# Two graph layers on one core: where the seven block products of a pair of row tiles stand among the adjacency matmuls of layer 0

## The chip, the core and the metric

The kernel runs on one core of a Trainium2 chip. The metric is the device time of one execution in microseconds (us). One more execution was taken by the hardware profiler; all rows quoted below are of that one. The engines are TensorE (PE; its weight loads are shown as PEld), VectorE (DVE), ScalarE (ACT), GpSimd (POOL) and SyncE (SP, which here only issues DMAs). PSUM is the accumulator memory that TensorE writes and ACT and DVE read.

## The reference

N = 3327 nodes, 1024 features. Two layers, each with a layer norm and a relu ahead of it and a residual sum behind it. Cut to what matters here:

```python
# layer 0
h = jnp.maximum(_layernorm(x), 0.0)
support   = relu(matmul(quant(h), quant(weight)) * scales)        # N x 1024
support_q = quant(support)
x = x + matmul(adj / asf, support_q / delta) * asf * delta        # (N x N) @ (N x 1024)
# layer 1: eight attention heads of 64 features, then four dense layers
h  = jnp.maximum(_layernorm(x), 0.0)
Wh = jnp.einsum('nf,hfd->hnd', h, W)                              # N x 512 over all heads
e  = leaky_relu(e_src[:, :, None] + e_dst[:, None, :])            # e_src = Wh . a1, e_dst = Wh . a2
att = softmax(where(adj > 0, e, -9e15))
enc = concat_heads(elu(att @ Wh))
x = x + dense4(enc)
```

The change lies in the product Wh = h W of layer 1, which the kernel computes during the adjacency product of layer 0.

## The kernel before

**Stages.** The rows are padded to 26 tiles of 128. First the support of layer 0 is made (to about 125 us). Then comes the adjacency stage (125.6 to 887.8 us), which is where the change is. Then attention over 8 heads and 4 groups of tiles, and at the end the dense layers.

**The adjacency stage** is a loop over the 26 row tiles t (line 820). For each, an accumulator `mm` of 128 x 1024 (two PSUM banks, two buffers) sums over the 26 column tiles j. Each adjacency block is split into a high part (`hi`, a cast by ACT, line 192) and a rest (`lo`, a subtraction by DVE, line 196), and each part is multiplied with both 512-column halves of `s_int[j]`: four matmuls for a j, 104 for a tile (line 849). The column tiles come in seven parts, `PARTS`: 0-3, 4-7, 8-11, 12-15, 16-19, 20-22, 23-25. A part is loaded by one DMA on SP's queue (line 188) into `at`; `at`, `hi` and `lo` have three buffers each, so the cast of a part waits until TensorE is done with the part three before it. DVE also makes the mask bytes `mk` from each part (line 197).

When a tile's sum is complete, ACT empties it (line 870), DVE scales it, adds it to x, measures it and normalises it (lines 871, 872, 148 to 153), ACT splits the row into two planes (line 626), two transposing DMAs on SP's queue turn it (line 628), and ACT joins the planes to `ht` (line 636). The next load of x and of adjacency parts stand behind those transposes in SP's queue.

**The pair of heads.** Wh for two neighbouring row tiles is computed in one 2 x 2 block product of Strassen's kind: seven block products in place of eight. `combined` (line 673) makes the sums of the stationary blocks on DVE, and `pair_of_heads` (line 693) is a generator that issues the seven products, the sums over them, and `closing_of_heads`. This happens in each even tile t from 2 to 24 (`paired`), for the tiles t-2 and t-1: 12 pairs.

A block product (`product`, line 704) is 4 float32 matmuls of 128 x 256, which the trace shows as 8 passes on TensorE. The results go to tiles `products` of one PSUM bank each (2 x 256 floats), two buffers. Product 1 opens a tile and product 2 takes its second half; 6 opens the second tile and 3 takes its second half; 7 opens one again (the first buffer) with 5 in its second half; 4 opens the second buffer again. Their readers:

- ACT copies product 1 to `p1` (line 718).
- DVE (line 716 is the helper `plus`) makes the first half of `wht` from p1 and product 2, then `u2` from p1 and product 6, then the second half of `wht` from u2 and product 3, then p1 anew from u2 and product 7, then adds product 5 to the second half.
- Then the tile t-2's rows are scaled and closed (line 730, `closing_of_heads` at line 790, with the scores, the exponentials on ACT, and the features `fw`, written by POOL's queue at line 813); the tile t-1's follow in the next tile.

**The order.** The instructions of an engine run in program order, and a scheduler sets that order from dependences and its own costs; `tc.keep_in_program_order` pins an instruction against its neighbours, and `queue_behind(ins, other)` (line 156) says that `ins` stands behind `other` in the engine's queue, with no semaphore.

In the loop over the parts n and their column tiles q, the generator is advanced (`next(steps)`) at (n, q) = (5, 1), (5, 2), (6, 0) and (6, 1). In the order that is built, product 1 stands behind the first column tile of part 5, and between the products stand adjacency matmuls, three and one in turn:

`1, three, 2, one, 6, three, 3, one, 7, three, 5, one, 4`

Of the kernel before, what the change touches and what calls it, by code (L numbers as in the profile page):

```python
# [28 lines left out]
KF = F // P  # L29
# [39 lines left out]
def two_layer_kernel(  # L69
# [23 lines left out]
    nc = tc.nc  # L93
# [34 lines left out]
    def load_rows(dst, ap, t):  # L128

        if rows_of(t) < P:  # L130
            nc.gpsimd.memset(dst, 0.0)
        for r in row_pieces(t):
            nc.sync.dma_start(dst[r], ap[t * P + r.start : t * P + r.stop, :])
# [22 lines left out]
    def queue_behind(ins, other):  # L156

        tc.add_manual_dep(
            ins.ins,
            other.ins.name,  # L160
            mybir.DependencyInfo(mybir.DependencyClass.NoSync, mybir.DependencyReason.DATA),
            reason="queue_behind",
        )
# [11 lines left out]
    with tc.tile_pool(name="at", bufs=2, reuse_waits="tile") as atp:  # L175
# [47 lines left out]
        with tc.tile_pool(name="s1", bufs=2, reuse_waits="tile") as s1, tc.tile_pool(  # L223
# [9 lines left out]
            def pin(ins):  # L233
                tc.keep_in_program_order(ins)

            def small_ps(name):
                return mm_ps.tile([P, F], F32, tag="mm", name=name)
# [106 lines left out]
            def product(t, c, k):  # L344
                if c == 0 and k == 0:
                    mms[t] = mm_ps.tile([P, F], F32, tag="mm", name="mm")
                r = slice(c * 512, (c + 1) * 512)
                pin(
                    nc.tensor.matmul(  # L349
                        mms[t][:, r], xqts[t][:, k, :], w_int[:, k, r], start=(k == 0), stop=(k == KF - 1)  # L350
                    )
                )
                if c == FC - 1 and k == KF - 1:
                    del xqts[t]
# [84 lines left out]
            ps = small_ps("w_meanp")  # L439
# [160 lines left out]
        with tc.tile_pool(name="differences", bufs=1, reuse_waits="tile") as dp, tc.tile_pool(  # L600
# [68 lines left out]
            def weight_differences():  # L669
                for d, one, other in ((t3, b22, b12), (b12, b12, b11), (t2, b22, b12), (t4, b21, t2)):  # L670
                    nc.vector.tensor_tensor(d, one, other, ALU.subtract)
# [21 lines left out]
            def pair_of_heads(t, of):  # L693

                r0, r1 = scales.pop(t), scales.pop(t + 1)
                wht = s2.tile([P, EMB], F32, name="wht", bufs=1)
                p1 = s2.tile([P, EMB // 2], F32, name="p1", bufs=1)
                u2 = s2.tile([P, NH, 2, HC], F32, tag="ft", name="u2", bufs=1)
                u2 = u2.rearrange("p h q c -> p (h q c)")[:, : EMB // 2]
                order = tc.keep_in_program_order  # L700
                half = slice(0, EMB // 2), slice(EMB // 2, EMB)
                banks = []

                def product(b):
                    st, mv = of[b]
                    if b in "1674":
                        banks.append(wh_ps.tile([P, 2, EMB // 2], F32, name="products"))
                    ps = banks[-1][:, int(b in "235")]
                    for k in range(KF // 2):
                        order(  # L710
                            nc.tensor.matmul(ps, st[:, k], mv[:, k], start=(k == 0), stop=(k == KF // 2 - 1))
                        )
                    return ps

                def plus(out, one, other):
                    nc.vector.tensor_tensor(out, one, other, ALU.add)

                order(nc.scalar.copy(p1, product("1")))
                plus(wht[:, half[0]], p1, product("2"))
                yield  # L720
                plus(u2, p1, product("6"))
                plus(wht[:, half[1]], u2, product("3"))
                yield
                plus(p1, u2, product("7"))
                of_5 = product("5")
                plus(wht[:, half[1]], wht[:, half[1]], of_5)
                yield
                of_4 = product("4")
                yield
                nc.vector.tensor_scalar(wht, wht, r0, None, ALU.mult)  # L730
                closing_of_heads(t, wht)
                yield
                wht = s2.tile([P, EMB], F32, name="wht", bufs=1)
                plus(wht[:, half[1]], p1, of_5)
                plus(wht[:, half[0]], p1, of_4)
                nc.vector.tensor_scalar(wht, wht, r1, None, ALU.mult)
                closing_of_heads(t + 1, wht)
                yield
# [77 lines left out]
                return products, powers  # L816

            hts, scales = {}, {}
            steps = iter(())
            for t in range(T):  # L820
                xt = s2.tile([P, F], F32, name="xt2", bufs=1)

                with tc.issue_after(turned.ins) if turned is not None else nullcontext():
                    load_rows(xt, x, t)
                mm = mm_ps.tile([P, F], F32, tag="mm", name="mm2")
                paired = t >= 2 and t % 2 == 0
                for n, js in enumerate(PARTS):
                    hi, lo = parts.pop(0)
                    parts.append(next(columns, None))
                    if n == 3:  # L830
                        for _ in steps:
                            pass
                    if js is PARTS[-1] and t - 2 in BATCHES:
                        rows_of_scores(t - 2)
                    if t == 1 and n == 0:
                        weight_differences()
                    if t > 0 and n == (3 if paired else 5):
                        join_planes(ht, parts_of_ht)
                        queue_behind(joins[0], highs[-1])
                    if paired and n == 3:  # L840
                        of = combined(t - 2)
                    for q, j in enumerate(js):
                        if paired and (n, q) == (5, 1):
                            steps = pair_of_heads(t - 2, of)
                        if paired and (5, 1) <= (n, q) <= (6, 1):
                            next(steps)
                        for which in (hi, lo):
                            for c in range(FC):
                                nc.tensor.matmul(  # L849
                                    mm[:, c * 512 : (c + 1) * 512],  # L850
                                    which[:, q, :],
                                    s_int[j][:, c * 512 : (c + 1) * 512],
                                    start=(j == 0 and which is hi),
                                    stop=(j == T - 1 and which is lo),
                                )
                if paired:
                    next(steps)
                if t == T - 2:
                    nc.gpsimd.dma_start(
                        b12, w_heads[: F // 2, EMB // 2 :].rearrange("(k p) e -> p k e", p=P)  # L860
                    )
                if t == 0:
                    for dst, ap in (
                        (whead, w_heads.rearrange("(k p) e -> p k e", p=P)),
                        (a1_t, a1.partition_broadcast(P)),
                        (a2_t, a2.partition_broadcast(P)),
                    ):
                        tc.keep_in_program_order(nc.sync.dma_start(dst, ap))
                y = s2.tile([P, F], F32, name="y", bufs=1)
                emptied = nc.scalar.activation(y, mm, AF.Copy, scale=r_asf)  # L870
                resumed = nc.vector.tensor_scalar(y, y, asf_t, sup_delta, ALU.mult, ALU.mult)
                nc.vector.tensor_tensor(xt, xt, y, ALU.add)
                nc.gpsimd.dma_start(x1_d[t * P : (t + 1) * P, :], xt)
                _, v = normalised(y, xt)
                r = half_inverse(v, "ln")
                lacking = nc.vector.tensor_scalar(r, r, 2.0, None, ALU.mult)
                if t == T - 1:
                    break
                ht, turned, parts_of_ht = transposed_by_dma(y, t)
                hts[t], scales[t] = ht, r  # L880
# [25 lines left out]
    with tc.tile_pool(name="over", bufs=2, reuse_waits="tile") as overp, tc.tile_pool(  # L906
# [18 lines left out]
        def load_features(h, js):  # L925
            r = slice(js[0], js[-1] + 1)
            return nc.sync.dma_start(
                (f_odd if h % 2 else f_even)[:, r], feat_d[r, h].rearrange("t p c -> p t c")
            )
# [148 lines left out]
        ins = load_features(0, range(8))  # L1078
        queue_behind(ins, scores)
        with tc.issue_after(ins.ins):  # L1080
            ins = load_mask(0, slice(TH, T))
        with tc.issue_after(ins.ins):
# [5 lines left out]
            ins = load_mask(3)  # L1088
# [404 lines left out]
```

## Time and profile before

| what | value |
|---|---|
| median of 3 runs | 2084.92 us (2084.8 to 2086.4) |
| the profiled execution's own time | 2085.89 us |
| its span, first to last instruction | 2084.1 us |
| adjacency matmuls, line 849 | 125.6 to 887.8 us |
| one adjacency matmul, median start to start | 0.227 us |
| block products, line 711 | 672 passes, 191.96 to 862 us |
| a tile without a pair / with a pair | 23.58 / 35.95 us |
| granted TensorE clock | 1.00 |

A row of the timeline gives the start in us from the span's start, how long the merged instructions ran, the engine, line and operation, what it writes and reads (`out<-in`), the shape, the count, and in brackets the idle time of the engine before it and what ended that. `PE` and `PEld` are the same engine; a weight load can run while a matmul streams. A row of the windows gives the window, its length, the busy time and count of PE, PEld, DVE, ACT and POOL in it, the granted clock, the DMA engines' busy share and GB/s.

Of the page's costliest groups, the two of the adjacency stage and the matmuls of the heads' pair stand like this (line, engine, operation, operands, count, busy us, mean ns, idle before):

```profile
L849 PE MATMUL mm<-s_int,lo 128*128 128x512 f32 x1352 | 429.5, 395 | 0.0
L849 PE MATMUL mm<-s_int,hi 128*128 128x512 f32 x1352 | 426.1, 396 | 0.0
```

A mean of 395 ns against a spacing of 227 shows that matmuls overlap: what counts is the spacing.

### The profile page before, as it was taken

What the parts mean: (1) busy time and instruction counts of PE and PEld (TensorE: products, weight loads), DVE (VectorE), ACT (ScalarE), POOL (GpSimd) and SP (SyncE); (2) the same over time, 40 slices, a digit from 0 to 9 for tenths busy, and PEclk for the clock granted to TensorE, in tenths of its full rate; (3) what the DMA queues carried; (4) which work ended last, traced back from release to release, by engine and by line L of the source; (5) the groups of instructions that cost most, each with busy time, mean ns of one, the idle gap of its engine ahead of it and who ended that gap; (6) DMA issues with size and microseconds to landing.
All of it is one profiled execution on the core that took longest, in us unless ns stands there. A gap on an engine that the chain in (4) does not pass through costs nothing.

```text
span 2084.1 us, 38595 instructions
## 1 busy us (share of the span) xinstructions
PE 2049.6 (98%) x15531; PEld 1742.2 (84%) x15541; DVE 1533.4 (74%) x3032; ACT 1337.0 (64%) x1828; POOL 183.1 (9%) x279
## 2 busy tenths in 40 slices
PE   5999999999999999999999999999999999999998
PEld 2468888888888888879999999999999999855554
DVE  8845676767666777687878777878778877757666
ACT  6733555444445554498888898888898888752321
POOL 2200000000020000111000000000000000000000
PEclk9999999999999999999999999999999999999999
DMA  6744554554455554592323224132324114544322
GB/s 222 177 146 139 169 161 147 147 144 140 149 166 169 161 151 147 148 374 88 97 59 114 67 66 118 42 112 64 118 66 117 41 43 123 115 110 132 116 86 76
DMA packets 202931, 261.98 MB, mean 126 GB/s; under 512 B 106020, under 2 KB 140948, under 8 KB 202752
## 3 DMA queue, kind: packets, MB, share of 16 engines
q1 hardware_dynamic: 183660, 191.08, 32.5%
q0 software_dynamic: 19024, 68.38, 10.4%
q8 instruction: 121, 1.98, 0.4%
q14 instruction: 58, 0.48, 0.1%
q10 hardware_dynamic: 68, 0.06, 0.0%
HBM read 155.90 MB, written 79.98 MB: 113 GB/s over the span
## 4 chain that ended last, share of the span: by engine, by line
PE 54%; ACT 1%; DVE 1%; issue 0%; DVEq 0%; ACTq 0%
PE acc L1019 41%; PE o L1402 7%; PE h_ps L1321 3%; PE h_ps L1290 1%; ACT over L990 1%; PE h_ps L1188 1%; PE whm L747 0%; DVE sel L999 0%; DVE sel L1000 0%; DVE su L1038 0%; DVE su L1043 0%; DVE prod L797 0%; ACT ht L1052 0%; DVE ft L779 0%; DVE stats L148 0%
## 5 line engine op out<-in xcount | busy, mean ns | idle before, releaser
L1019 PEld LDWEIGHTS <-sel 128*128 128x128 fp8e4 x10816 | 910.6, 98 | 8.4 <-issue 3.8
L990 ACT ACTIVATE over<-srow,large_dst 128x896 uint8<-128x896 f32 (+1 forms) x766 | 683.2, 974 | 12.5 <-DVE sel L999 12.4
L1019 PE MATMUL acc<-f_even,sel 128*128 128x195 bf16 x5408 | 458.6, 248 | 2.1 <-DVE sel L1000 0.9
L1019 PE MATMUL acc<-f_odd,sel 128*128 128x195 bf16 x5408 | 456.7, 248 | 0.0
L849 PE MATMUL mm<-s_int,lo 128*128 128x512 f32 x1352 | 429.5, 395 | 0.0
L849 PE MATMUL mm<-s_int,hi 128*128 128x512 f32 x1352 | 426.1, 396 | 0.0
L999 DVE TENSOR_TENSOR sel<-over,mask 128x448 uint32<-128x448 uint32 (+1 forms) x416 | 243.8, 586 | 160.3 <-ACT over L990 130.4
L849 PEld LDWEIGHTS mm<-s_int,lo 128*128 128x128 f32 x1352 | 253.8, 188 | 52.5
L849 PEld LDWEIGHTS mm<-s_int,hi 128*128 128x128 f32 x1352 | 253.8, 188 | 51.9
L1000 DVE TENSOR_TENSOR sel<-sel,mask 128x448 uint32<-128x448 uint32 (+1 forms) x416 | 245.9, 591 | 14.2
L192 ACT CAST hi<-at 128x512 fp32r<-128x512 f32 (+1 forms) x182 | 105.6, 587 | 153.2 <-PE mm L849 95.7
L196 DVE TENSOR_TENSOR lo<-at,hi 128x512 fp32r<-128x512 f32 (+1 forms) x182 | 117.7, 647 | 35.3 <-ACT hi L192 33.8
L1052 ACT ACTIVATE ht<-su,rs 128x64 f32<-128x64 f32 x208 | 53.2, 335 | 106.4 <-DVE rs L1048 106.4
L1067 POOL DMA_DIRECT2D enc_d<-eh x64 | 57.7, 906 | 717.0 <-ACT eh L1065 716.5
L1038 DVE TENSOR_REDUCE su<-acc 128x130 f32<-128x390 f32 x208 | 115.6, 556 | 4.8 <-PE acc L1019 4.8
L349 PE MATMUL mm<-w_int,xqt 128*128 128x512 bf16 x406 | 93.3, 383 | 7.1 <-DVE w_int L480 4.5
L626 ACT COPY yh<-y 128x1024 uint16<-128x1024 uint16 x50 | 51.9, 1038 | 57.0 <-DVE y L151 57.0
L349 PEld LDWEIGHTS <-xqt 128*128 128x128 bf16 x416 | 40.4, 99 | 55.3 <-issue 8.8
L636 ACT COPY ht<-yht 128x1024 uint16<-128x1024 uint16 x50 | 67.6, 1357 | 25.4 <-DMA yht<-yh 25.1
L197 DVE TENSOR_SCALAR mk<-at 128x512 uint8<-128x512 f32 (+1 forms) x182 | 72.4, 398 | 0.0
L1043 DVE SCALAR_TENSOR_TENSOR su<-su,ratio 128x65 f32<-128x65 f32 x208 | 59.7, 287 | 7.4
L803 ACT ACTIVATE ratio<-srcs 128x8 f32<-128x8 f32 x26 | 5.4, 209 | 88.2 <-DVE srcs L798 88.2
(291 smaller groups left out, 2075.3 us busy)
## 6 DMA issues: line engine op xcount, KB each, us to landing
at<-in_adj_t SPq DMA_DIRECT2D x130, 256.0 KB, 3.1
feat_d<-fw POOLq DMA_DIRECT2D x24, 800.0 KB, 6.1
x_d<-xt POOLq DMA_DIRECT2D x26, 512.0 KB, 3.5
xb<-x_d SPq DMA_DIRECT2D x26, 512.0 KB, 3.6
x_d<-xb POOLq DMA_DIRECT2D x26, 512.0 KB, 3.4
nodes<-x_d SPq DMA_DIRECT2D x26, 512.0 KB, 4.7
xt<-in_x SPq DMA_DIRECT2D x25, 512.0 KB, 4.2
out<-yo SPq DMA_DIRECT2D x50, 256.0 KB, 2.1
```

Of the source, the lines that this page charges most:

```text
L192: ins = high = nc.scalar.copy(hi, at)
L196: low = nc.vector.tensor_tensor(lo, at, hi.bitcast(F32), ALU.subtract)
L197: ins = nc.vector.tensor_scalar(mk[:, r], at, 0.0, float(EDGE), ALU.is_gt, ALU.mult)
L349: nc.tensor.matmul(mms[t][:, r], xqts[t][:, k, :], w_int[:, k, r], start=(k == 0), stop=(k == KF - 1))
L636: nc.scalar.copy(halves_of_words(ht[:, c * KF // FC : (c + 1) * KF // FC].rearrange("p k i -> p (k i)")), yht.rearrange("p (two k) i -> p ...
L849: nc.tensor.matmul(mm[:, c * 512 : (c + 1) * 512], which[:, q, :], s_int[j][:, c * 512 : (c + 1) * 512], start=(j == 0 and which is hi), s ...
L990: nc.scalar.activation(over[:, q], srows[i], AF.Relu, bias=large_dst[:, j, h : h + 1], scale=BIG)
L999: pin(nc.vector.tensor_tensor(up, over, of_pair, ALU.bitwise_and))
L1000: ends["vector"] = pin(nc.vector.tensor_tensor(dn, up, of_pair, ALU.bitwise_xor))
L1019: ins = nc.tensor.matmul(accs[i, b][:, r], chosen[i, pair][:, s, b, q], f[:, j, s * FS : s * FS + FW // 2], start=(j == 0 and s == 0), sto ...
L1038: nc.vector.tensor_reduce(su[:, b], accs.pop((i, b)).rearrange("p (q s c) -> p q c s", q=2, s=3), AX.X, ALU.add)
L1402: nc.tensor.matmul(ps, st[:, k, q // 2], mv[:, k], start=(k == 0), stop=(k == 1))
```

## The change

In `pair_of_heads` the three `yield`s between the products go, so that one advance of the generator issues all seven. That advance stands at (n, q) = (5, 2), ahead of the last column tile of part 5. The block products' matmuls are collected in a list, and the high matmuls of that column tile and of the first column tile of each later part are queued behind the last of them. The sums over the products, the closing of the two tiles and everything else are as they were.

```diff
@@ pair_of_heads
-                order = tc.keep_in_program_order
...
                     for k in range(KF // 2):
-                        order(
-                            nc.tensor.matmul(ps, st[:, k], mv[:, k], start=(k == 0), stop=(k == KF // 2 - 1))
+                        block_products.append(
+                            tc.keep_in_program_order(
+                                nc.tensor.matmul(ps, st[:, k], mv[:, k], start=(k == 0), stop=(k == KF // 2 - 1))
+                            )
                         )
...
-                order(nc.scalar.copy(p1, product("1")))
+                tc.keep_in_program_order(nc.scalar.copy(p1, product("1")))
                 plus(wht[:, half[0]], p1, product("2"))
-                yield
                 plus(u2, p1, product("6"))
                 plus(wht[:, half[1]], u2, product("3"))
-                yield
                 plus(p1, u2, product("7"))
                 of_5 = product("5")
                 plus(wht[:, half[1]], wht[:, half[1]], of_5)
-                yield
                 of_4 = product("4")
                 yield
@@ the loop over the tiles
             hts, scales = {}, {}
+            block_products = []
...
                     for q, j in enumerate(js):
-                        if paired and (n, q) == (5, 1):
+                        if paired and (n, q) == (5, 2):
                             steps = pair_of_heads(t - 2, of)
-                        if paired and (5, 1) <= (n, q) <= (6, 1):
                             next(steps)
                         for which in (hi, lo):
                             for c in range(FC):
-                                nc.tensor.matmul(
+                                ins = nc.tensor.matmul(
...
+                                if block_products and which is hi and (q == 0 or (n, q) == (5, 2)):
+                                    queue_behind(ins, block_products[-1])
```

In the order that is built, product 1 stands behind the second column tile of part 5, and the seven products follow one another with nothing between them; the last column tile of part 5 and part 6 come behind product 4. The waits written on products 2 (for ACT), 6, 3 and 5 (for DVE) are the same as before. On DVE, the low part and mask of the next tile's second part move from among the sums to behind the first three operations of the closing, and the low parts of its fourth and fifth parts move ahead of the normalisation of the row. On ACT the cast of the next tile's third part moves ahead of the emptying of the sum. On POOL's queue two of the mask loads at the end of the stage move behind the feature write of tile 22, and the feature write of tile 23 ahead of a write of scores.

## The prediction

> **What bounds the kernel now.** I read the page's busy line first, then the busy time by window for one tile with a pair in it and one without, then the timeline of that pair on all engines, then what waits for what.
>
> ```profile
> span 2084.1 us, 38595 instructions
> PE 2049.6 (98%) x15531; PEld 1742.2 (84%) x15541; DVE 1533.4 (74%) x3032; ACT 1337.0 (64%) x1828; POOL 183.1 (9%) x279
> ```
>
> ```profile
> 232.45:268.40 35.95, 35.95 (x161) 29.92 (x160) 19.45 (x41) 12.66 (x17) 2.21 (x3) 1.00 0.48 135
> 268.40:291.98 23.58, 23.58 (x105) 19.52 (x104) 21.36 (x44) 16.93 (x25) 2.34 (x3) 1.00 0.62 182
> 125.60:887.80 762.20, 762.20 (x3381) 632.45 (x3379) 512.59 (x1035) 363.73 (x509) 68.54 (x97) 1.00 0.54 154
> ```
>
> In the window rows the second figure is PE's busy time. Over the whole of layer 0's adjacency stage (125.6 to 887.8 us) TensorE has no idle time. A tile without a pair takes 23.58 us for its 104 adjacency matmuls, 0.2267 each; the tile with a pair takes 35.95, so the pair's block products cost 12.37. Whatever lengthens TensorE's stream here moves the end by as much: nothing in this stage can pay it back, as TensorE waits nowhere else in it.
>
> The timeline of that pair (products in the order 1, 2, 6, 3, 7, 5, 4):
>
> ```profile
> 251.49 1.89 PE L711 MATMUL products<-whead,ht 128*128 128x256 f32 x8
> ...
> 253.03 0.81 PE L849 MATMUL mm<-s_int,hi 128*128 128x512 f32 x2
> 253.42 0.37 ACT L718 COPY p<-products 128x256 f32<-128x256 f32 x1 [2.46 <-PE products L711]
> ...
> 253.68 0.40 PE L849 MATMUL mm<-s_int,lo 128*128 128x512 f32 x1
> 253.84 1.59 PEld L711 LDWEIGHTS products<-whead,ht 128*128 128x128 f32 x8 [0.20 <-ACT p L718]
> 253.91 1.92 PE L711 MATMUL products<-whead,ht 128*128 128x256 f32 x8
> ...
> 255.90 1.89 PE L711 MATMUL products<-differences,s 128*128 128x256 f32 x8
> ...
> 257.83 0.42 DVE L716 TENSOR_TENSOR u<-p,products 128x256 f32<-128x256 f32 x1 [1.46 <-PE products L711]
> ...
> 258.30 1.59 PEld L711 LDWEIGHTS products<-whead,s__2469 128*128 128x128 f32 x8 [0.26 <-DVE u L716]
> 258.32 1.98 PE L711 MATMUL products<-whead,s__2469 128*128 128x256 f32 x8
> ...
> 262.77 1.59 PEld L711 LDWEIGHTS products<-whead,s 128*128 128x128 f32 x8 [0.26 <-DVE p L716]
> ```
>
> The reader is to see three weight loads that stand still until ACT or DVE has read the product before: 2 waits for the copy of 1, 3 for the sum that reads 6, 5 for the sum that reads 7. Each of these shares an accumulator tile with the product it follows. Between the two stand three adjacency matmuls, 3 x 0.2267 = 0.68 us, which cover nearly all of the wait.
>
> **The change part by part.** *The three covers go.* One product is 8 passes (x8). Its 1.89 us run from the start of the first to the end of the last, and one pass alone lasts 0.379, so passes start every (1.89 - 0.379)/7 = 0.2158 us, and a product takes 1.726 of TensorE's time. Seven make 12.08 us; the 0.285 that the pair costs above that is three waits not quite covered (1.92 and 1.98 against 1.89: 0.03 + 0.09 + 0.09 = 0.21) and about 0.075 for 14 changes between the two kinds of matmul.
>
> In the changed order the seven follow one another, still with the waits at 2, 3 and 5. The full length of each wait is in the same rows. Product 1's last pass starts at 251.49 + 7 x 0.2158 = 253.00, so a next pass could start at 253.22; ACT's copy ends at 253.79, the weights load from 253.84, and the first pass effectively starts 0.03 after its record, at 253.95: 0.73 us. Product 6: last pass at 257.41, next possible 257.63, DVE's sum ends 258.25, load 258.30, effective start 258.32 + 0.09 = 258.41: 0.78. Product 7 to 5: the same, 0.78. Sum 2.29 us. The other three changeovers wait for nothing: 6 goes to a free accumulator, 7 needs the sum of 1 and 2, which ends some 3.6 us sooner, 4 needs the sum with 3, done some 3.6 us sooner.
>
> So a pair costs 12.08 + 2.29 + two changes of kind (about 0.01) = 14.38 in place of 12.37: +2.01 us. There are 12 pairs: +24.1 us.
>
> A bound for these waits from below: if the weights of the waiting product were in place already, each would be shorter by the 0.11 us between the first and the second load after the wait, 36 x 0.11 = 4.0 us in all. From above: one mask instruction of DVE (L197, 0.42 us) in front of one of the sums, 12 x 0.42 = 5.0. I take the measured waits, because the same semaphore ends them in both kernels and DVE is idle before each sum (1.46 us before the one above).
>
> The Trainium skill, "TensorE: Matmul & The Clock Gate", section "Step-by-step: what each phase is for", says that TensorE pulls weight loads ahead of running matmuls. The rows above show 0.20 and 0.26 us in which the load of the waiting product did not go ahead, so the wait holds it too; by the rule the sum would be some 4 us smaller, about 2106.
>
> *The moved instructions.* Product 1 starts two adjacency matmul pairs (0.91 us) later, so all that reads block products starts at the same place or later than before while the tile's end is 2.0 us later: the sums end 4.7 us ahead of the tile's end (3.2 before), no new cost. The adjacency matmuls behind the piece release their high and low parts later, so the casts for the next tile's second part, in ACT's and DVE's queues behind the pair's copy and sums, run at about 267.4 in place of 258.28; TensorE wants them at 274.0. In DVE's order the pair's sums go ahead of that part's low half, and two later low halves and one mask move ahead of the normalisation (L151). From the starts of the rows, L871 to L151 was 6.39 us and becomes 6.39 + 0.60 + 0.29 = 7.28, so the normalised row, its two transposes and, behind them in SP's queue, the next xt load and adjacency loads are 0.9 to 1.0 us late relative to TensorE. The cover: the first part of tile 6 was cast by 288.58 and wanted at 291.98, 3.4 us; some 2.4 remain. In POOL's queue tile 22's feature write, which waits for DVE until 872, goes ahead of two mask loads that stood at 870 to 871: some 3 us later, first wanted by the selection at 893.30. Nothing.
>
> Only at the end of layer 0 is that cover already gone:
>
> ```profile
> 886.37 1.36 ACT L636 COPY ht<-yht 128x1024 uint16<-128x1024 uint16 x1 [3.67 <-DMA yht<-yh]
> ```
>
> The last-but-one tile's head products start at 887.78, as soon as this copy ends (887.73). A row that is 1.0 us late delays them by that, once: +1.0 us (0 to 1.6). The chain of waits goes through TensorE there, so it reaches the end.
>
> *Queueing later adjacency matmuls behind the block products* adds order, no semaphore: 0.
>
> *The clock.* New gaps of 0.73 to 0.78 us stand in TensorE's stream, three within 14 us.
>
> ```profile
> 28.30:100.00 71.70, 67.91 (x352) 31.79 (x358) 63.60 (x157) 54.21 (x61) 19.60 (x44) 1.00 0.65 170
> ```
>
> Here TensorE is idle 3.8 us out of 71.7, with one gap of 1.3 us at 68 us, and the granted clock stays at 1.00. So I take 0. The same page, section "A second HAM failure mode: psum-queue depth-cycling", tells of short idle times between groups of matmuls that make the clock fall to half; its window is 3.4 us, and by that rule an estimate is 1.7 us lost a pair, 20 us in all, about 2130.
>
> *Sum:* 24.1 + 1.0 = 25.1 us. The profiled execution has a span of 2084.1 and took 2085.89, 1.8 us around the span; the median of the runs is 2084.92. The span becomes 2109.2, the median 2110.0.
>
> **The rivals.**
> - *Not slower: the accumulators come free at once.* If the waits at 2, 3 and 5 were only the lateness of ACT and DVE behind other work, a piece would cost 12.08 + 0.01 and save 0.28 us a pair: -3.3 us, 2081.6. It decides only if the three waits together stay under 0.28 us. Against it: ACT and DVE start 0.04 us after the product's last pass ends, and the copy or sum alone takes 0.37 or 0.42. For it: only that the order of products is unchanged and was covered.
> - *The adjacency is late.* If the casts of the next tile's first part come 1 us too late (the 2.4 us cover misjudged by 3.4), TensorE waits in each pair's next tile: 12 us more, 2122. For it: ACT already waits 0.78 us for that load at 287.96. Against it: the margin.
> - *All six changeovers wait*, because each accumulator's release is told late: 3 x 0.78 more a pair, 28 us more, 2138. Against it: the sums that free them end 3.6 us sooner.
>
> **How the numbers follow.** Forecast 0.87, not slower 0.04, adjacency late 0.06, all six 0.03. Time: 2110.0. Range: down by 4.0 (weights in place) and 1.0 (no carry at the end of the layer), 2105; up by 5.0 and 0.6, 2115.5; outside it lies about 0.17. What a measurement can tell from no change is about 0.2%, 4.2 us: faster (under 2080.7) 0.01, same 0.04, slower 0.95.
>
> **What would show it.** Paired tiles of 37.96 us and odd tiles still of 23.58; PE idle before products 2, 3 and 5 of 0.7 to 0.8 us and none at 6, 7 and 4; layer 0's matmuls ending 24 us later; the granted clock at 1.00. Wrong if the piece takes under 13 us, if matmuls of L847 wait for casts, or if the loss of layer 0 doesn't arrive at the end.

## The result, and the profile after

The changed kernel takes 2110.91 us (median of 4 runs, 2108.6 to 2111.86) against 2085.55 for the kernel before beside it (4 runs, 2084.8 to 2086.4): a ratio of 1.012, with a 95% interval of 1.0102 to 1.0137. It is slower by 25.4 us; 25.1 had been forecast.

The profiled execution of after has a span of 2110.1 us. Its busy line, from the page:

```profile
span 2110.1 us, 38606 instructions
PE 2056.9 (97%) x15531; PEld 1742.9 (83%) x15541; DVE 1530.3 (73%) x3032; ACT 1336.7 (63%) x1828; POOL 179.4 (9%) x279
```

The same number of matmuls as before, 26.0 us more of span, of which the page counts 7.3 as PE busy and the rest as idle. Of the 26.0, 24.4 lie in the adjacency stage of layer 0; this profile also enters that stage 2.55 us later than the one of before, with a granted clock of 0.98 ahead of it (28.3 to 125 us; 1.00 in before), and is 1.0 us shorter behind it. The busy time by window, for the same pair's tile, the tile that follows it, and the whole adjacency stage of layer 0 (window, its length, PE busy, PEld, DVE, ACT, POOL, granted clock, DMA share, GB/s):

```profile
237.08:275.05 37.97, 36.49 (x162) 29.91 (x160) 20.37 (x45) 13.04 (x20) 2.43 (x3) 1.00 0.42 120
275.05:298.62 23.57, 23.57 (x105) 19.52 (x104) 20.86 (x41) 16.41 (x23) 2.02 (x4) 1.00 0.64 192
128.12:914.76 786.64, 768.78 (x3381) 632.61 (x3380) 510.80 (x1036) 364.90 (x510) 65.10 (x97) 1.00 0.52 149
```

The odd tile is what it was; the paired tile has gone from 35.95 to 37.97, and has idle time on PE that it did not have. All twelve paired tiles lie between 37.97 and 38.00. The stage has gone from 762.24 to 786.64 us, +24.40 by the ends of its matmuls, while PE's busy time in it has grown by 6.6: the stage lost its time in waits, of which the profile shows 17.9 us as idle and counts the rest as busy. The clock is 1.00 in each row.

Where the idle time sits is in the timeline of that pair (start, duration, engine, line, operation, and in brackets the idle time before it with its releaser):

```profile
257.02 1.89 PE L711 MATMUL products<-whead,ht 128*128 128x256 f32 x8
258.95 0.37 ACT L719 COPY p<-products 128x256 f32<-128x256 f32 x1 [3.37 <-PE products L711]
259.37 1.59 PEld L711 LDWEIGHTS products<-whead,ht 128*128 128x128 f32 x8 [0.86 <-ACT p L719]
259.37 1.99 PE L711 MATMUL products<-whead,ht 128*128 128x256 f32 x8 [0.46 <-ACT p L719]
261.20 1.89 PE L711 MATMUL products<-differences,s 128*128 128x256 f32 x8
263.13 0.42 DVE L717 TENSOR_TENSOR u<-p,products 128x256 f32<-128x256 f32 x1 [1.24 <-PE products L711]
263.61 1.99 PE L711 MATMUL products<-whead,s__2469 128*128 128x256 f32 x8 [0.51 <-DVE u L717]
265.44 1.89 PE L711 MATMUL products<-differences,ht 128*128 128x256 f32 x8
267.84 1.99 PE L711 MATMUL products<-whead,s 128*128 128x256 f32 x8 [0.51 <-DVE p L717]
269.67 1.89 PE L711 MATMUL products<-differences,ht 128*128 128x256 f32 x8
```

Seven products, in the order 1, 2, 6, 3, 7, 5, 4. Those with a bracket are 2, 3 and 5, the ones that write the other half of an accumulator that ACT or DVE is still reading. They last 1.99 instead of 1.89: with the semaphore the weight load starts at the same moment as the matmul, and its 0.10 us are part of the wait. So product 2 really starts at 259.47, 2.45 after product 1, where a product takes 1.726: a wait of 0.73. By the same reading product 3 waits 0.78 and product 5 0.77. The page's 0.46 and 0.51 are smaller because the last pass's end and the load don't count as idle.

### The profile page after: what moved, and what is told of

The parts are those of the page before. It is cut to its first block, busy times and chain, and to the rows that moved or that the text cites. A ratio compares the mean times of both kernels' runs of the same rounds, so it can differ in the third digit from the quotient of the medians.

```text
span 2110.1 us, 38606 instructions
## 1 busy us (share of the span) xinstructions
PE 2056.9 (97%) x15531; PEld 1742.9 (83%) x15541; DVE 1530.3 (73%) x3032; ACT 1336.7 (63%) x1828; POOL 179.4 (9%) x279
## 3 DMA queue, kind: packets, MB, share of 16 engines
q0 software_dynamic: 19024, 68.38, 10.2%
## 4 chain that ended last, share of the span: by engine, by line
PE 53%; ACT 2%; DVE 1%; issue 0%; DVEq 0%; ACTq 0%
PE acc L1019 40%; PE o L1402 7%; PE h_ps L1321 3%; ACT over L990 1%; PE h_ps L1290 1%; PE h_ps L1188 1%; DVE su L1038 0%; DVE sel L999 0%; DVE sel L1000 0%; DVE ft L777 0%; DVE su L1043 0%; ACT fw L785 0%; ACT ht L1052 0%; DVE prod L795 0%; DVE over L984 0%
## 5 line engine op out<-in xcount | busy, mean ns | idle before, releaser
L990 ACT ACTIVATE over<-srow,large_dst 128x896 uint8<-128x896 f32 (+1 forms) x766 | 683.1, 974 | 13.6 <-DVE sel L999 12.5
L847 PE MATMUL mm<-s_int,hi 128*128 128x512 f32 x1352 | 419.1, 391 | 0.0
L847 PE MATMUL mm<-s_int,lo 128*128 128x512 f32 x1352 | 416.5, 389 | 0.0
L847 PEld LDWEIGHTS mm<-s_int,lo 128*128 128x128 f32 x1352 | 253.8, 188 | 53.0
L847 PEld LDWEIGHTS mm<-s_int,hi 128*128 128x128 f32 x1352 | 253.7, 188 | 52.8
L626 ACT COPY yh<-y 128x1024 uint16<-128x1024 uint16 x50 | 51.9, 1038 | 61.0 <-DVE y L151 61.0
L717 DVE TENSOR_TENSOR wht<-p,products 128x256 f32<-128x256 f32 x36 | 13.9, 414 | 56.5 <-PE products L711 56.5
```

The lines of the kernel that those rows point to most:

```text
L847: ins = nc.tensor.matmul(mm[:, c * 512 : (c + 1) * 512], which[:, q, :], s_int[j][:, c * 512 : (c + 1) * 512], start=(j == 0 and which is hi),
L990: nc.scalar.activation(over[:, q], srows[i], AF.Relu, bias=large_dst[:, j, h : h + 1], scale=BIG)
```

## The experiments

In the order in which they ran; "stage" is layer 0's adjacency stage, from its first matmul to the end of its last, "behind" what follows it. Times in us; each ratio is to the kernel before, run in turn on the same chip, where its median was 2086.29 beside e1 to e4, 2086.33 beside e5 to e8 and 2086.45 beside e9.

| kernel | paired tile | stage | behind | median | ratio, 95% interval |
|---|---|---|---|---|---|
| before | 35.93 to 35.96 | 762.24 | 1196.31 | 2085.55 | |
| after | 37.97 to 38.00 | 786.64 | 1195.30 | 2110.91 | 1.012, 1.0102 to 1.0137 |
| e1, order 1 6 2 3 7 4 5 | 35.67 | 758.85 | 1198.41 | 2085.95 | 1.0, 0.9991 to 1.0009 |
| e2, order 1 6 2 3 7 5 4 | 36.45 to 36.47 | 768.28 | 1196.82 | 2093.8 (one run) | |
| e3, one sum made twice | 38.43 to 38.45 | 792.03 | 1196.08 | 2117.11 (one run) | |
| e4, nothing queued behind | 35.93 to 37.74 | 766.57 | 1194.79 | 2089.85 | 1.0017, 1.0008 to 1.0026 |
| e5, before again | 35.94 to 35.96 | 762.27 | 1195.28 | 2086.02 (one run) | |
| e6, e1 with masks moved | 35.67 | 758.83 | 1196.08 | 2084.20 | 0.9987, 0.9978 to 0.9996 |
| e7, before with masks moved | 35.95 to 35.96 | 762.26 | 1197.77 | 2088.37 | 1.0009, 1.0 to 1.0018 |
| e8, e4 at the earlier place | 35.93 to 35.95 | 761.94 | 1196.07 | 2086.56 | 0.9998, 0.9989 to 1.0007 |
| e9, e6 with features first | 35.67, one 35.85 | 759.03 | 1199.67 | 2087.82 | 1.0007, 0.9998 to 1.0016 |

The time ahead of the stage is the same program in all, and lies between 125.57 and 128.12 in these profiles. The two that enter the stage last, after and e1, have a granted clock of 0.98 ahead of it, all others 1.00. Before and before again differ by 1.1 there and by 1.0 behind the stage. Differences of that size between two profiles are therefore not explained here.

**e1: the same piece, in an order in which no product follows the one that it shares a bank with.**

```
-                banks = []
+                banks = {}
...
-                        banks.append(wh_ps.tile([P, 2, EMB // 2], F32, name="products"))
-                    ps = banks[-1][:, int(b in "235")]
+                        banks[b] = wh_ps.tile([P, 2, EMB // 2], F32, name="products")
+                    ps = banks[{"2": "1", "3": "6", "5": "7"}.get(b, b)][:, int(b in "235")]
...
-                plus(wht[:, half[0]], p1, product("2"))
                 plus(u2, p1, product("6"))
+                plus(wht[:, half[0]], p1, product("2"))
                 plus(wht[:, half[1]], u2, product("3"))
                 plus(p1, u2, product("7"))
+                of_4 = product("4")
                 of_5 = product("5")
                 plus(wht[:, half[1]], wht[:, half[1]], of_5)
-                of_4 = product("4")
```

> The changed kernel with the products in the order 1, 6, 2, 3, 7, 4, 5 (same piece, same place, same queueing; 2, 3 and 5 write the second half of the bank opened by 1, 6 and 7 as before). Now another product of 1.73 us stands between each pair that shares a bank. Theory (three waits for the reader of the first half, 0.73 + 0.78 + 0.78 us a pair): no wait is left, the paired tile takes 23.58 + 12.08 + 0.01 = 35.67 us, 2.32 less than the changed kernel's 37.99, 12 pairs 27.9 us less: about 2083, 3 us under the kernel before. Rival (the piece as such costs, by its place or by what is late behind it): it stays near 2110.

The same pair in e1, TensorE's timeline:

```profile
254.61 1.89 PE L711 MATMUL products<-whead,ht 128*128 128x256 f32 x8
256.34 1.89 PE L711 MATMUL products<-differences,s 128*128 128x256 f32 x8
258.06 1.89 PE L711 MATMUL products<-whead,ht 128*128 128x256 f32 x8
259.79 1.89 PE L711 MATMUL products<-whead,s__2469 128*128 128x256 f32 x8
261.52 3.62 PE L711 MATMUL products<-differences,ht 128*128 128x256 f32 x16
264.97 1.89 PE L711 MATMUL products<-whead,s 128*128 128x256 f32 x8
```

No bracket is left: a product every 1.72 or 1.73 us, two of them in one record of 16 passes. The stage is 27.8 us shorter than after's. So the piece costs nothing by being in one piece; the three hand-overs of a bank cost it all. The paired tile is 0.28 us below that of before, which is the 0.285 that the prediction found above pure passes in the old order. But the 3.4 us that the stage wins over before do not reach the end (ratio 1.0): behind the stage, e1 takes 2.1 us more than before, 3.1 more than before again.

**e2: the same, with 5 directly behind 7.** Against e1, `of_5` and its sum stand ahead of `of_4` again, so one wait comes back.

> As the first, but 5 directly behind 7 and 4 last: one of the three waits comes back. Theory: only product 5 waits, 0.78 us a pair, 9.4 us over the order 1, 6, 2, 3, 7, 4, 5, paired tile 36.46 us, about 2092. Rival (a wait moves to where there is most to wait for, so that one is as long as three): near 2110.

```profile
261.17 1.89 PE L711 MATMUL products<-differences,ht 128*128 128x256 f32 x8
263.57 1.99 PE L711 MATMUL products<-whead,s 128*128 128x256 f32 x8 [0.51 <-DVE p L717]
```

One bracket in the pair (TensorE's timeline of e2), 0.78 to 0.80 us a paired tile, 9.43 us over the stage; three such waits are 28.3 against the 27.8 that e1 took away. The waits add up one by one.

**e3: the sum that frees product 6's bank is made twice.**

```
-                plus(u2, p1, product("6"))
+                of_6 = product("6")
+                plus(u2, p1, of_6)
+                plus(u2, p1, of_6)
```

> The changed kernel with the sum of product 6 made twice by DVE, one behind the other, the same result. Theory: product 3's weight load waits for the last reader of product 6, so that wait grows by one sum and its hand-over, 0.42 to 0.48 us, 12 pairs: 5.0 to 5.8 us over the changed kernel, about 2116, and the waits at 2 and 5 stay. Rival (the wait is a fixed time that TensorE needs between two products of one bank): no change, about 2111.

The pair in e3, DVE and the weight load of product 3:

```profile
262.61 0.88 DVE L717 TENSOR_TENSOR u<-p,products 128x256 f32<-128x256 f32 x2 [1.24 <-PE products L711]
263.54 1.59 PEld L711 LDWEIGHTS products<-whead,s__2470 128*128 128x128 f32 x8 [1.37 <-DVE u L717]
```

DVE's 0.46 us more are TensorE's 0.46 us more: the idle time before product 3 grows from 0.91 to 1.37, the stage by 5.39 = 12 x 0.45. DVE has time enough here (1.24 us idle before it starts); what counts is how long its reading of the bank takes.

**e4: after without the queueing of later adjacency matmuls.**

```
-                                if block_products and which is hi and (q == 0 or (n, q) == (5, 2)):
-                                    queue_behind(ins, block_products[-1])
```

> The changed kernel without queueing later adjacency matmuls behind the block products; the order that is built then has three adjacency matmuls between 1 and 2, between 6 and 3 and between 7 and 5, and none elsewhere. Theory: the covers are back, each wait is down to 0.03 to 0.10 us, a paired tile takes 35.9 us and the time is that of the kernel before, 2083.5 to 2086. Rival (one advance of the generator at the later place costs by itself): near 2110, or in between.

In the order as built, three adjacency matmuls stand between 1 and 2, between 6 and 3 and between 7 and 5 again, and none elsewhere. The stage is 20.1 us shorter than after's, and eight of the paired tiles have before's 35.9. Without the two queueing lines other matmuls slip into the gaps, whatever the source says of one piece, and no product of a paired tile shows a wait any more. But the stage is still 4.3 us longer than before's, which was not expected: the kernel takes 2089.85, above the upper end of the theory. Four paired tiles take 36.47, 36.88, 37.13 and 37.74. One of them, first ACT and then TensorE in e4's timeline:

```profile
473.05 0.62 ACT L192 CAST hi<-at 128x512 fp32r<-128x512 f32 x1 [2.51 <-DMA at<-in_adj_t]
...
479.68 0.60 ACT L192 CAST hi<-at 128x512 fp32r<-128x512 f32 x1
485.71 1.05 ACT L626 COPY yh<-y 128x1024 uint16<-128x1024 uint16 x1 [5.42 <-DVE y L151]
...
489.11 1.03 ACT L192 CAST hi<-at 128x512 fp32r<-128x512 f32 x2
...
489.78 0.73 PE L847 MATMUL mm<-s_int,hi 128*128 128x512 f32 x2 [0.98 <-ACT hi L192]
```

The lateness begins at the adjacency loads: the cast of this tile's first part stands 2.51 us for its load. Behind it in ACT's order come feature casts that DVE needs, then the copy of the normalised row, for which ACT stands 5.42 us, and only then the casts that TensorE needs next. The same holds for another of the four, with the cast at 291.52:

```profile
291.52 0.62 ACT L192 CAST hi<-at 128x512 fp32r<-128x512 f32 x1 [3.39 <-DMA at<-in_adj_t]
```

In the four long tiles the first part is cast 0.22, 0.80, 1.08 and 1.49 us before TensorE wants it, in the other eight 1.99 us or more. TensorE does not wait there yet; it waits at the fifth part, whose cast stands behind the row. This is the prediction's second rival, the late adjacency, in a kernel that is not after. The later place alone does not bring it, for e1 has that place too, a pair still shorter, and no such wait (its least lead is 1.32 us); there the piece is closed. e8 below has the piece drawn apart at the old place.

**e5: before again**, for the spread between two profiles of one program.

> The kernel before once more, for a second profile of it. If the 125.6 us ahead of the adjacency stage and the 1196.3 us behind it vary by themselves, as they do between the profiles of the other kernels (126.8 to 128.1 and 1194.8 to 1198.4), this one lies inside those, and the 2.55 us by which the changed kernel's stage began later is no part of the change. If 125.6 is the kernel's own, it is 125.6 again. The stage itself: 762.2 us both ways.

The stage repeats within 0.03 us, what lies around it within 1.1.

**e8: e4 with the piece at its old place**, to tell the place from the piece: `(5, 2)` becomes `(5, 1)`.

> The changed kernel without the queueing, as in the fourth experiment, with the seven products one column tile earlier, where the kernel before has them. In the fourth experiment four of the twelve paired tiles were 0.5 to 1.8 us longer because ScalarE's casts came late. Theory (the later place takes 0.9 us of the lead that the loads behind the row's transposes have): no paired tile is longer than 36.0 us, about 2086. Rival (one advance of the generator puts DVE's order so that the row is late): the same long tiles, about 2090.

Every paired tile takes 35.93 to 35.95, TensorE waits for no cast, and the time is before's (0.9998), though the normalised row is 1.1 us later after a paired tile than in before. So the three generator stops that the change takes out are worth nothing either way. e4's 4.6 us more of stage than e8's come from the later place, and, with e1, only where the piece is also drawn apart. That this is because the piece then ends later is not shown, nor why the loads come late.

**Why e1's gain did not reach the end: e6, e7 and e9.** The first attention matmuls need a selection, and the first selection (`over`, L990 in after and e1) stands in ACT's order behind the two copies that end the last transposed rows. ACT in e1, at the end of layer 0:

```profile
885.34 1.35 ACT L636 COPY ht<-yht 128x1024 uint16<-128x1024 uint16 x1 [5.39 <-DMA yht<-yh]
...
891.63 3.84 ACT L990 ACTIVATE over<-srow,large_dst 128x896 uint8<-128x896 f32 x4
```

and in before:

```profile
891.29 3.84 ACT L990 ACTIVATE over<-srow,large_dst 128x896 uint8<-128x896 f32 x4
```

Against the end of the stage (886.88 and 887.80) the selection is later in e1: it comes 4.75 us after it, in before 3.48 and in before again 2.42. In before, after, e1, e4, e5 and e8 alike the 61st attention matmul comes 11.25 or 11.26 us after this first selection, so what moves it moves the first attention matmuls. Of the 2.1 us that e1 takes longer than before behind the stage, 1.3 are there at the selection; the other 0.8 come behind the 61st matmul and are not explained.

What makes the selection late is only in part seen. ACT stands 5.39 us for the last-but-one tile's transposes. The last of these lands 9.1 us after its issue in e1, beside seven mask loads that POOL issues, but that is no longer than in the two profiles of before (9.8 and 7.5). What is later in e1 is the row itself: its copy (L626) starts 12.78 us ahead of the stage's end, in both profiles of before 14.71 or 14.70. The same holds in the paired tiles ahead: from tile 6 to tile 22 the copy starts 10.8 us after the tile's end in e1, 9.6 in after and 8.9 in before. It is later than in before in every run with one advance of the generator (9.4 in e4, 10.0 in e8), and latest with e1's order; what puts it back on DVE was not followed up, and no run brings it forward. Instead, e6 takes e1 and moves the mask loads to SP's queue, behind the score row:

```
-        load_mask(0, slice(0, TH), nc.gpsimd)
...
+        with tc.issue_after(scores.ins):
+            load_mask(0, slice(0, TH))
```

> The order 1, 6, 2, 3, 7, 4, 5 and, at the end of layer 0, the first seven mask loads taken from GpSimd's queue and put into SyncE's behind the last row's transposes and the first score row. Theory (attention begins a fixed 11.26 us after ScalarE's first selection, which stands behind the join of those transposes; in the first experiment the mask loads ran beside them, the second one took 9.1 us to land, and the 3.4 us won in the stage were lost there): the transposes land 3 to 4 us after their issue, the first selection comes 2 to 3 us earlier, and the total is 2080 to 2083, less than both kernels. Rival (the selections wait for the masks, which now come later): no gain, 2085 to 2089.

ACT, DVE and TensorE in e6:

```profile
878.83 1.35 ACT L636 COPY ht<-yht 128x1024 uint16<-128x1024 uint16 x1
...
886.08 3.84 ACT L990 ACTIVATE over<-srow,large_dst 128x896 uint8<-128x896 f32 x4 [0.86 <-DMA srow<-src_d]
...
891.72 0.62 DVE L999 TENSOR_TENSOR sel<-over,mask 128x448 uint32<-128x448 uint32 x1 [5.37 <-DMA mask<-mask_d]
```

The transposes land after 3.1 us, ACT doesn't wait for them, and the selection starts 0.20 us after the stage instead of 4.75. But now DVE stands 5.37 us for the masks, and TensorE 3.0 us for the features; the 61st attention matmul comes 15.5 us after the selection, no longer 11.25. What is left is a gain: 2084.20 us against 2086.33, a ratio of 0.9987 (0.9978 to 0.9996). The gain is small, but this version beats both kernels.

e7 makes the mask move alone, in before:

> The kernel before with the mask loads moved in the same way and nothing else. Theory: the adjacency stage stays at 762.2 us and the part behind it is 1 to 3 us shorter, 2083 to 2085.5. Rival (it is the stage's length that sets when the selections begin): unchanged, 2086.

Neither came: 2088.37, 2.0 us slower than before's 2086.33, with an interval that just reaches 1.0. ACT's first selection comes 0.13 us after the stage, but DVE's first (`sel`) only 7.58 us after it, in before 5.49. The move is no gain by itself; it paid only with e1's order. e9 is e6 with the first features loaded ahead of the masks:

```
-        with tc.issue_after(scores.ins):
-            load_mask(0, slice(0, TH))
         ins = load_features(0, range(8))
         queue_behind(ins, scores)
+        with tc.issue_after(ins.ins):
+            ins = load_mask(0, slice(0, TH))
```

where the first `ins` is the feature load's, so that the masks go behind it.

> As the sixth experiment, with the first feature load ahead of the seven mask loads in SyncE's queue: there the first attention matmul stood 3.0 us waiting for that load (it began 9.88 us after the stage, 6.7 in the kernel before). Theory: it begins at 7 to 8 us, the part behind the stage is 1 to 2 us shorter than the 1196.1 of the sixth, the total 2082 to 2083.5. Rival (the first selection waits for the masks in any case, 5.4 us in the sixth, and they land 0.4 us later now): no change from 2084.2.

That did not come either: 2087.82, 3.6 us slower than e6. DVE's first selection in e9:

```profile
896.21 0.62 DVE L999 TENSOR_TENSOR sel<-over,mask 128x448 uint32<-128x448 uint32 x1 [9.75 <-DMA src_d<-srct]
```

It starts 4.5 us later than in e6, after 9.75 us of idleness that ends with a DMA. Moving these loads shifts the wait between transposes, masks and features. Which order is best there stays open.

## Why the prediction was right, step by step

**TensorE's stream decides, and nothing in the stage pays back: right.** The stage grew by 24.40 us and the runs by 25.36.

**The three covers go, +2.01 us a pair: right.** Measured +2.04 on the mean of the twelve tiles. The waits were foreseen as 0.73, 0.78, 0.78 and are 0.73, 0.78, 0.77; e1 takes all of them away by order alone (-27.8 us, where 12 x 2.29 is 27.5), e2 puts one back, e3 lengthens one by what its reader lengthens.

**The bound below, weights in place early, -4.0: not taken, rightly.** The Trainium skill, "TensorE: Matmul & The Clock Gate", section "Step-by-step: what each phase is for", has the loads pulled ahead of running matmuls. Here the load of a waiting product does not go ahead: it starts in the same moment as its matmul (259.37 and 259.37), after 0.86 us without a load.

**The moved instructions, no cost in the stage: right.** No matmul of L847 waits in after, and the odd tiles are as long as before. The last sum of the pair above ends at 270.29, 4.8 us ahead of the tile's end, where 4.7 were foreseen. The cover was misjudged, on the safe side: the lead of tile 6's first part was to shrink from 3.4 to some 2.4 us, and it is 3.8 in after. It had been read from one tile; the least in before is 1.76 us, in tile 12. e4 shows that the late adjacency was a real danger all the same: 4.6 us at the same place, with the piece drawn apart. The cover that the prediction counted gives way first there, but the price is paid at the fifth part's cast, behind the row in ACT's order, at which the prediction did not look.

**+1.0 us at the end of layer 0: this step failed.** The row is 0.7 us late relative to the end of the stage (its copy starts 13.98 us ahead of it, in before 14.71), near the 0.9 to 1.0 foreseen. But the wait that I saw in one profile, the last-but-one tile's head products behind the copy of 886.37, is not there in after. ACT in after:

```profile
907.40 1.36 ACT L636 COPY ht<-yht 128x1024 uint16<-128x1024 uint16 x1 [0.59 <-DMA yht<-yh]
...
914.10 1.34 ACT L636 COPY ht<-yht 128x1024 uint16<-128x1024 uint16 x1 [4.41 <-DMA yht<-yh]
...
917.62 3.84 ACT L990 ACTIVATE over<-srow,large_dst 128x896 uint8<-128x896 f32 x4 [1.10 <-DMA srow<-src_d]
```

The first copy is done 6 us before the stage ends at 914.76; it is the second that waits, and what it delays is the first selection, 2.86 us after the stage against 3.48 in before and 2.42 in before again. The part behind the stage is 1.0 us shorter than in before and the same as in before again (1195.30 and 1195.28). So the profiles show no such cost beyond the spread of one program, and what can be late there is the selection rather than the head products. The median of after exceeds that of before by 1.0 us more than the stage explains. That is the size of the term, but the interval of the difference (21.3 to 28.6 us) is far too wide to show it. So 24.4 us of the difference are accounted for, against 24.1 in the sum; that the total of 25.1 came within 0.3 us of the medians is in part luck.

**Queueing adds order, no semaphore, 0: right as a sentence about semaphores, wrong as an account.** By e4, without these lines the covers are back and the waits gone, and the stage is 20.1 us shorter in spite of 4.3 us for late casts: the lines keep the covers out. The working had put the whole price on the covers, so the sum was not hurt. A reader who takes it for the price of those lines would undo the wrong part.

**The clock, 0: right.** It is 1.00 in the adjacency stage and behind it, with 36 stops of 0.46 to 0.51 us, three within 9 us; the 0.98 ahead of the stage comes before the first of them. The estimate of about 2130 drew on the Trainium skill, "TensorE: Matmul & The Clock Gate", section "A second HAM failure mode: psum-queue depth-cycling"; no run here shows anything of it.

**The rivals.** Not slower: e1 gives its 35.67 us a pair, but only in another order; in the order of after the accumulators do not come free at once. All six changeovers: 6, 7 and 4 show no bracket.

## What to carry to other kernels

A matmul that writes the other half of an accumulator tile waits until the last reader of the first half is done: here 0.73 to 0.78 us, the reader's 0.37 to 0.42 plus hand-over and weight load. The wait is a semaphore that the program carries; no run here gives each product a bank of its own. Put one independent product between the two, and the wait is gone with no other work needed; three other matmuls as filler take away nearly all of it as well, so look at what really stands in the gaps before taking them out. This stage, which fills TensorE, lost every such wait in full. The gain of e1 did not reach the end, where the next stage's first inputs did not come earlier too.

## What the runs showed of the hardware that was not expected

The last transposing DMA of layer 0 landed 3.1 to 3.4 us after its issue in e6, e7 and e9, but 6.5 to 10.2 us after it in the eight other profiles, where seven mask loads from POOL's queue run beside it. From e1 to e6 it gained 6 us, and DVE's first selection then stood 5.4 us for the masks.

TensorE's rows under-report a wait of this kind: 0.51 us as idle where 0.78 are lost, because the pass that ends and the weight load that starts lie outside it. The distance between two starts, less the time of a product, gives the true price.
